# Where the router products stand in query group 0, where weight sums 0 and 1 and the rows are built, and which queue stores the value sums

## The chip, the core and the metric

The kernel runs on one core of one Trainium2 chip. The metric is device time in microseconds of one execution, the median of several. Everything is fp32. A core has a matrix engine (TensorE, PE in the profile), VectorE (DVE), ScalarE (ACT), GpSimd (POOL) and a queue engine (SyncE, SP). Each engine works through its own list of instructions in order; SP, ACT and POOL can also issue DMA transfers, and a transfer that has to wait for its data holds up what stands behind it in that engine's list.

## The reference, cut to what matters

x has 4096 rows of 512, the context 3202 rows of 512. The first part is an attention of the normed rows over the context, whose result, with its products with the rows, is mixed by W_qv; the second is a mixture of experts.

```python
Sim = (hc @ w1)[:, :, None] + (ctx @ w2)[:, None, :] + einsum('bid,bjd->bij', hc * w3, ctx) + b_sim
A = softmax(Sim, axis=2)
hq_hat = einsum('bij,bjd->bid', A, ctx)
Batt = softmax(max(Sim, axis=2), axis=1)
hc_bar = einsum('bi,bid->bd', Batt, hc)
feats = concatenate([hc, hq_hat, hc * hq_hat, hc * hc_bar])
x = x + tanh(g_xattn) * (feats @ W_qv + b_qv)
...
logits = layernorm(x) @ w_router + b_router        # top 2 of 8 experts, capacity 1280
x = x + tanh(g_ffn) * moe(layernorm(x))
```

## The kernel before, in words

Stage 1 does the attention in eight groups of 512 queries (g = 0 to 7). In each group `stage_s` makes the similarities E of all context rows, in six steps jj of two pairs of context tiles each, and keeps a running maximum M on DVE. Products of two by two blocks are done with seven block products instead of eight (`chain`, and `seven` in stage 3), which needs sums of blocks on both sides; DVE builds them. For the keys they are stored to kt_d in group 0 and loaded in later groups; for the values they are stored to vs_d and vd_d (`left_sums`, `build_rest_values`); for the mixing weights W_qv to wt_d (`build_weights(c)`, c = 0 to 3: two loads of wc, the copy of the router columns we into it, a store of wc, four sums wt, a store of wt, both stores on POOL).

At the end of `stage_s` the maximum over all keys is taken: DVE finishes M, PE transposes it in four pieces (mps, L566), DVE reduces it to mt and spreads it on a diagonal (dgm), PE multiplies this with ones (mbps, L159), ACT copies the result to mb, DVE subtracts mb from E (L602), ACT takes the exponent (L603). In groups 1 to 7 the first products of `stage_d(g - 1)`, the mixing of the group before (pad, p6d and so on, with the weights wp loaded from wt_d), stand in this wait on PE.

In group 0 there is no group before. There, 64 router products, W_qv times the centred router weights (we, L289: 128x128 weights, 8 columns), are handed out by the generator `beside`: `behind(mm, beside, n)` issues the next n of them behind the matmul mm. Before the change 12 stand ahead of the transposes, 12 behind them, 24 behind mbps, and the last 16 one by one behind value products. They read W_qv from tiles that borrow the space of others (wq2 lies where xr, the rows of x for the mixing, lies later).

In group 0 the values are not built yet, so `stage_v` multiplies with the plain context tiles: 13 steps j (12 pairs of tiles vc and a rest), each pair with eight products of 512 columns (vv, L677), into four banks. Beside this DVE makes the value sums of step j from vc (vsv), and the store to vs_d goes out from POOL. The tiles vs, wt and vd share a ring of two buffers (tag "vs"), so every third one waits until a store has landed. vc and kt tiles share a ring of five (tag "st"); SP loads them in order. Also in this stage: `stage_n(1)` (statistics of the next queries, after j = 3; POOL stores means to mr_d and loads them back as mrb), `stage_a(1)` (the right side Qp of the next group and its sums), and `stage_z(0)` (ebb and four sums jz). At the end ACT copies the four banks to hqT.

Group 1 then runs `stage_s(1)`, and `rest_rows` (jj = 0), `left_operand` (jj = 1, with the rows xr: four loads, four additions of bqv and a copy of be) and `build_weights(0)` to `(3)` (jj = 1 to 4) are worked in between on DVE. `stage_d(0)`, which needs wt_d, begins at the end of `stage_s(1)`. Before it SP issues 12 zero stores to buf_d.

Stages 2 (routing) and 3 (experts) are not touched.

The order on an engine is mostly set by a planner, which picks by cost and due time; `tc.issue_after(...)` ties an instruction behind another one. The calls around the change are these:

Of the kernel before, what the change touches and what calls it, by code (L numbers as in the profile page):

```python
# [6 lines left out]
F32 = mybir.dt.float32  # L7
I32 = mybir.dt.int32
AF = mybir.ActivationFunctionType
ALU = mybir.AluOpType  # L10
# [4 lines left out]
P = 128  # L15
# [5 lines left out]
def gated_layer(ctx, tc, x, x_t, ctxt, ctxt_t, ctxt_c, ctxt_r, g_xattn, g_ffn, w_sim, w_sim_r, b_sim, W_qv, W_qv_t, b_qv, b_qv_c, w_router, b_router, w1, b1, w2, b2, out):  # L21
# [6 lines left out]
    nc = tc.nc  # L28
# [4 lines left out]
    DC = D // P  # L33
# [90 lines left out]
    with ExitStack() as s1:  # L124
# [218 lines left out]
        def stage_a(g, qT, mrb, last, exp):  # L343

            with tc.issue_after(last.ins):
                tt(qT, qT, mrb[:, 0, :].unsqueeze(1).to_broadcast([P, DC, TG]), ALU.subtract)
            tt(qT, qT, mrb[:, 1, :].unsqueeze(1).to_broadcast([P, DC, TG]), ALU.mult)
            Qp = sb.tile([P, DC, TG], F32, name=f"Qp{g}", tag="Qp")
            with tc.issue_after(exp.ins):
                for c in range(DC):  # L350
                    nc.scalar.activation(
                        Qp[:, c, :], qT[:, c, :], AF.Identity,
                        scale=ws[:, 2 * DC + c : 2 * DC + c + 1], bias=ws[:, DC + c : DC + c + 1],
                    )
                nc.scalar.dma_start(qT_d[g], qT)
            right_sums(g, qT, Qp)
# [33 lines left out]
        def left_sums(name, vc, dst):  # L390

            vs = sb.tile([P, 4, 256], F32, name=f"vs{name}", tag="vs", bufs=2)
            A11, A21, A12, A22 = (vc[:, h, c : c + 256] for h in range(2) for c in (0, 256))
            tt(vs[:, 0, :], A21, A22, ALU.add)
            tt(vs[:, 1, :], vs[:, 0, :], A11, ALU.subtract)
            tt(vs[:, 2, :], A11, A21, ALU.subtract)
            total = tt(vs[:, 3, :], A12, vs[:, 1, :], ALU.subtract)
            nc.gpsimd.dma_start(dst, vs)
            return total
# [5 lines left out]
        def build_rest_values(vc):  # L405
            vd = sb.tile([P, 256], F32, name="vd", tag="vs", bufs=2)
            tt(vd, vc[:, :256], vc[:, 256:], ALU.subtract)
            nc.gpsimd.dma_start(vd_d, vd)

# [78 lines left out]
        def stage_s(g):  # L488
# [8 lines left out]
            for jj, js in enumerate(PAIRS):  # L497
# [28 lines left out]
                if g == 1:  # L526
                    with tc.issue_after(e_add.ins):
                        if live["then"]:
                            live["then"].pop(0)()
                        if 0 < jj <= DC:  # L530
                            build_weights(jj - 1)
                if jj == 4 and 0 < g < NG - 1:
# [23 lines left out]
            if g == 0:  # L556
# [4 lines left out]
                live[g]["pw"] = pw  # L561
            mm = behind(mm, beside, 12)
            ps = ps_tr.tile([P, 4, P], F32, name=f"mps{g}", tag="tr")
            for i in range(4):
                with tc.issue_after(mm.ins):
                    mm = nc.tensor.transpose(ps[:, i, :], M[:, i // 2, 0, (i % 2) * P : (i % 2 + 1) * P], ident)  # L566
            mm = behind(mm, beside, 12)
            mt = sm.tile([P, 4], F32, name=f"mt{g}", tag="mt")
# [3 lines left out]
            with tc.issue_after(mm.ins):  # L572
                mm = diag_rows(ps, f"m{g}", mt)
            live[g]["beside"], live[g]["mm"] = beside, behind(mm, beside, 24)

# [71 lines left out]
        def stage_v(g, early, between):  # L647
# [8 lines left out]
            def product(ps, what, right, start=True, stop=True, rest=None, right_c=None):  # L656
                for i in range(2):
                    vt = load_values(g, what, i, rest)
                    js = list(range(i * JH, (i + 1) * JH)) + ([NJ] if i and rest is not None else [])
                    for j in js:  # L660
                        for b in range(2):
# [4 lines left out]
                            )  # L666

            if g == 0:

                beside, mm = v["beside"], v["mm"]  # L670
                ps = [bank(f"vv{b}") for b in range(DC)]
                for j in range(NJ + 1):
# [9 lines left out]
                    with tc.issue_after(v["last"].ins):  # L682
                        if j < NJ:
                            total = build_values(j, vc)
                        else:
                            build_rest_values(vc[:, 0, :])
                    if j == 2:
                        with tc.issue_after(v["last"].ins):
                            nc.vector.tensor_copy(we, v["pw"])
# [3 lines left out]
                    if j == 5:  # L693
                        early()
                    if j == 8:
                        v["sums"] = total
                assert next(beside, 0) == 0
                for b in range(DC):
# [74 lines left out]
            def left_operand():  # L773
# [8 lines left out]
                v["A"] = {"1": A11, "6": S2, "7": A21, "5": S1, "2": A12, "4": A22, "3": S4}  # L782
                xr = sb.tile([P, 4, 2, BW], F32, name=f"xr{g}", tag="xr")
                for i in range(4):
                    t = 4 * g + i
                    with tc.issue_after(queue[-1].ins):
                        nc.sync.dma_start(xr[:, i, :, :256], x[t * P : (t + 1) * P, :].rearrange("p (j d) -> p j d", j=2))
                    with tc.issue_after(v["last"].ins):
                        tt(xr[:, i, :, :256], xr[:, i, :, :256], bqv.rearrange("p (j d) -> p j d", j=2), ALU.add)
                with tc.issue_after(v["last"].ins):  # L790
                    nc.vector.tensor_copy(
                        xr[:, :, :, 256:],
                        be.rearrange("p (j e) -> p j e", j=2).unsqueeze(1).to_broadcast([P, 4, 2, BW - 256]),
                    )
                v["x"] = xr

            if g:
                rest_rows()
                left_operand()
            else:  # L800

                live["then"] = [rest_rows, left_operand]
# [24 lines left out]
        def stage_z(g):  # L827

            v = live[g]
            ebb = v["ebb"]  # L830
            with tc.issue_after(v["exp"].ins):
                nc.scalar.activation(ebb, ebb, AF.Copy, accum_out=hz[:, g, DC : DC + 1])
# [695 lines left out]
```

## Time and profile before

| | us |
|---|---|
| median of 3 runs | 2652.79 (2651.25 to 2656.39) |
| the profiled execution | 2650.92 |
| its span | 2649.1 |
| PE busy | 2598.4 |
| DVE busy | 1703.0 |
| ACT busy | 458.6 |
| POOL busy | 234.6 |

The span is the time from the first to the last instruction of the profiled execution; the rest of its time lies around it. Busy times of different engines overlap. Times in the timelines are microseconds from the start of the span. In them the wait for maxima of group 0 runs from 94 to 112 us, the value products of group 0 from 112 to 204, the similarities of group 1 from 204 to 282, and the mixing of group 0 begins after that. PE splits each fp32 matmul into two, so 24 router products are 48 lines of the timeline.

### The profile page before, as it was taken

How to read it: one execution, taken by the hardware profiler on the slowest of the kernel's cores; microseconds unless marked ns; L12 is line 12 of the kernel's file. 1: busy time of each engine (PE TensorE's matmuls, PEld its weight loads, DVE VectorE, ACT ScalarE, POOL GpSimd, SP SyncE). 2: the span in 40 equal slices, each digit the busy share in tenths (PEclk: the TensorE clock that was granted, in tenths of full speed). 3: DMA queues.
4: the chain of work that ended last, by engine and by line, in shares of the span. 5: the costliest groups of instructions: out<-in, count | busy, mean ns of one | idle time of the engine just before them, and what ended most of it. 6: DMA issues, size and time to landing. Idle time of an engine off the chain costs nothing. (4 is left out here: it accounts for less than half of the span.)

```text
span 2649.1 us, 29673 instructions
## 1 busy us (share of the span) xinstructions
PE 2598.4 (98%) x11200; PEld 2101.7 (79%) x11200; DVE 1703.0 (64%) x3430; ACT 458.6 (17%) x788; POOL 234.6 (9%) x301
## 2 busy tenths in 40 slices
PE   8999999999999999999999996999999999999998
PEld 7748888888888888888888885777777777777776
DVE  7857856947758578568465566574747565565654
ACT  1201200201102002012020143111111111111111
POOL 0010100000001000000000065010101010101010
PEclk9899999999999999999999997999999999999999
DMA  8576765746746657467446794232314232223210
GB/s 317 175 207 236 217 216 168 242 158 184 251 153 178 242 162 241 169 175 249 149 136 215 271 357 173 74 115 72 128 64 138 95 117 88 104 88 104 76 60 20
DMA packets 178255, 436.06 MB, mean 165 GB/s; under 512 B 17454, under 2 KB 77998, under 8 KB 176064
## 3 DMA queue, kind: packets, MB, share of 16 engines
q1 hardware_dynamic: 150208, 352.25, 40.2%
q0 software_dynamic: 17872, 51.46, 6.1%
q10 hardware_dynamic: 10032, 30.46, 2.9%
q8 instruction: 88, 1.44, 0.2%
q14 instruction: 55, 0.45, 0.1%
HBM read 355.71 MB, written 85.55 MB: 167 GB/s over the span
## 5 line engine op out<-in xcount | busy, mean ns | idle before, releaser
L1276 PE MATMUL pah<-bT,w 128*128 128x320 f32 x512 | 161.1, 437 | 0.5 <-ACT p1h L1283 0.5
L512 PE MATMUL pas<-Qp,kt 128*128 128x256 f32 x672 | 160.3, 380 | 0.0
L662 PE MATMUL pbv<-E,vt 128*128 128x256 f32 x672 | 147.3, 379 | 0.0
L662 PEld LDWEIGHTS pbv<-E,vt 128*128 128x128 f32 x672 | 127.7, 190 | 17.3
L512 PEld LDWEIGHTS pas<-Qp,kt 128*128 128x128 f32 x672 | 127.2, 190 | 17.4 <-issue 0.5
L1276 PEld LDWEIGHTS pah<-bT,w 128*128 128x128 f32 x512 | 98.2, 192 | 40.5 <-ACT p1h L1283 1.4
L602 DVE TENSOR_TENSOR E<-E,mb 128x1024 f32<-128x1024 f32 x96 | 115.2, 1215 | 14.0 <-ACT mb L589 14.0
L603 ACT ACTIVATE E<-E 128x1024 f32<-128x1024 f32 x96 | 101.5, 1058 | 129.3 <-DVE E L602 128.0
L1276 PE MATMUL pao<-w,h 128*128 128x256 f32 x512 | 121.0, 379 | 0.0
L1459 POOL DMA_INDIRECT out<-acc,ti x40 | 40.9, 1022 | 865.1 <-DVE dc L1325 531.2
L1047 PE MATMUL x1p<-W,q2T 128*128 128x264 f32 x512 | 116.1, 387 | 0.0
L1436 PE MATMUL op<-w,h 128*128 128x512 f32 x256 | 114.8, 592 | 0.0
L1276 PEld LDWEIGHTS pao<-w,h 128*128 128x128 f32 x512 | 97.3, 190 | 20.0 <-issue 7.7
L1047 PEld LDWEIGHTS x1p<-W,q2T 128*128 128x128 f32 x512 | 96.7, 190 | 16.1
L468 ACT COPY p1s<-pas 128x512 f32<-128x512 f32 x48 | 28.1, 585 | 437.1 <-issue 257.1
L538 DVE TENSOR_TENSOR M<-M,E 128x1024 f32<-128x1024 f32 x80 | 97.8, 1223 | 4.1
L677 PE MATMUL vv<-E,vc 128*128 128x512 f32 x192 | 88.2, 610 | 0.0
L1436 PEld LDWEIGHTS op<-w,h 128*128 128x128 f32 x256 | 46.6, 190 | 48.7 <-issue 41.4
L1398 DVE TENSOR_TENSOR h<-p4h,u3h 128x320 f32<-128x320 f32 x64 | 31.3, 489 | 78.3 <-PE p4h L1276 78.3
L481 ACT COPY E<-pas 128x512 f32<-128x512 f32 x48 | 28.1, 585 | 306.5 <-PE pas L512 296.7
L1276 PE MATMUL p6h<-x,w1s 128*128 128x320 f32 x256 | 80.2, 436 | 0.0
L512 PE MATMUL pbs<-Qp,kt 128*128 128x256 f32 x336 | 79.7, 380 | 0.3 <-DVE E L479 0.3
(449 smaller groups left out, 5390.3 us busy)
## 6 DMA issues: line engine op xcount, KB each, us to landing
kt<-kt_d SPq DMA_DIRECT2D x84, 896.0 KB, 4.7
w<-in_w SPq DMA_DIRECT2D x32, 2048.0 KB, 9.1
vt<-vs_d SPq DMA_DIRECT2D x56, 768.0 KB, 7.2
wp<-wt_d SPq DMA_DIRECT2D x56, 520.0 KB, 4.6
kt_d<-ktb ACTq DMA_DIRECT2D x12, 896.0 KB, 5.5
buf_d<-zero SPq DMA_DIRECT2D x80, 129.0 KB, 6.0
xb<-buf_d SPq DMA_DIRECT2D x40, 258.0 KB, 6.6
r<-r_d SPq DMA_DIRECT2D x32, 260.0 KB, 6.0
```

The source lines that it names most:

```text
L468: nc.scalar.copy(p1, pa)
L512: nc.tensor.matmul(ps[:, jl, :], kts[j][:, KSLOT[p], k, :], B[p][:, k, :], start=start and jl == 0 and k == 0, stop=stop and k == 1, skip_ ...
L538: tt(M, M, e[:, :, h], ALU.max)
L602: live[g]["last"] = tt(e, e, m, ALU.subtract)
L603: live[g]["exp"] = nc.scalar.activation(e, e, AF.Exp)
L662: nc.tensor.matmul(ps[b], vt[:, j - i * JH, b * P : (b + 1) * P], right(j) if j < NJ else right_c, start=start and j == 0 and b == 0, stop ...
L677: mm = nc.tensor.matmul(ps[b], vc[:, h, b * P : (b + 1) * P], E[j // 2][:, :, h, j % 2, :] if j < NJ else ec, start=j == 0 and h == 0, sto ...
L1047: mm = nc.tensor.matmul(ps[:, j, :B1], qTs[g][:, c, q * P : (q + 1) * P], W1[:, c, j, :], start=(c == 0), stop=(c == DC - 1))
L1276: nc.tensor.matmul(ps, a, b, start=start and i == 0, stop=stop and i == len(A) - 1, skip_group_check=True)
L1398: tt(hi[:, :HC], ps, u, ALU.add)
L1436: nc.tensor.matmul(ps, hT[:, k, 2 * MH :], W2[:, k, :], start=(k == 0), stop=(k == KH - 1))
L1459: sc = nc.gpsimd.indirect_dma_start(out=out[:, :], out_offset=rows_of(ti, s), in_=acc[:, :], in_offset=None, bounds_check=N - 1, oob_is_er ...
```

## The change

Of the 64 router products 6, 7 and 8 stand at the three places of the wait for maxima, and 43 one by one behind the first 43 value products; their result is copied to we after j = 5 instead of j = 2. The rows xr with their bias become a function of their own, which group 0 calls at j = 6 of its value stage (the other groups call it where it stood). `build_weights(0)` and `(1)` are called at j = 7 and 9 of the value stage; `build_weights(2)` and `(3)` at jj = 1 and 2 of group 1. The stores of value sums go out from ACT's queue instead of POOL's. The copy of ebb in group 0 is tied behind the store of qT_d.

```diff
@@ -352,7 +352,7 @@
                         Qp[:, c, :], qT[:, c, :], AF.Identity,
                         scale=ws[:, 2 * DC + c : 2 * DC + c + 1], bias=ws[:, DC + c : DC + c + 1],
                     )
-                nc.scalar.dma_start(qT_d[g], qT)
+                live["sent"] = nc.scalar.dma_start(qT_d[g], qT)
             right_sums(g, qT, Qp)
 
         def build(j):
@@ -395,7 +395,7 @@
             tt(vs[:, 1, :], vs[:, 0, :], A11, ALU.subtract)
             tt(vs[:, 2, :], A11, A21, ALU.subtract)
             total = tt(vs[:, 3, :], A12, vs[:, 1, :], ALU.subtract)
-            nc.gpsimd.dma_start(dst, vs)
+            nc.scalar.dma_start(dst, vs)
             return total
 
         def build_values(j, vc):
@@ -405,7 +405,7 @@
         def build_rest_values(vc):
             vd = sb.tile([P, 256], F32, name="vd", tag="vs", bufs=2)
             tt(vd, vc[:, :256], vc[:, 256:], ALU.subtract)
-            nc.gpsimd.dma_start(vd_d, vd)
+            nc.scalar.dma_start(vd_d, vd)
 
         def build_weights(c):
 
@@ -527,8 +527,8 @@
                     with tc.issue_after(e_add.ins):
                         if live["then"]:
                             live["then"].pop(0)()
-                        if 0 < jj <= DC:
-                            build_weights(jj - 1)
+                        if 0 < jj <= DC - 2:
+                            build_weights(jj + 1)
                 if jj == 4 and 0 < g < NG - 1:
                     ahead[g + 1] = stage_n(g + 1)
                 if jj == 0:
@@ -559,19 +559,19 @@
                 pw = pw.rearrange("p (k c e) -> p k c e", k=4, c=DC)
                 beside = live[g]["we"](pw, [1, 2, 0, 3])
                 live[g]["pw"] = pw
-            mm = behind(mm, beside, 12)
+            mm = behind(mm, beside, 6)
             ps = ps_tr.tile([P, 4, P], F32, name=f"mps{g}", tag="tr")
             for i in range(4):
                 with tc.issue_after(mm.ins):
                     mm = nc.tensor.transpose(ps[:, i, :], M[:, i // 2, 0, (i % 2) * P : (i % 2 + 1) * P], ident)
-            mm = behind(mm, beside, 12)
+            mm = behind(mm, beside, 7)
             mt = sm.tile([P, 4], F32, name=f"mt{g}", tag="mt")
             nc.vector.tensor_reduce(mt, ps, AX.X, ALU.max)
             tt(mt, mt, left[g][1], ALU.max)
             ps = ps_tr.tile([P, 4, P], F32, name=f"mbps{g}", tag="tr").rearrange("p a b -> p (a b)")
             with tc.issue_after(mm.ins):
                 mm = diag_rows(ps, f"m{g}", mt)
-            live[g]["beside"], live[g]["mm"] = beside, behind(mm, beside, 24)
+            live[g]["beside"], live[g]["mm"] = beside, behind(mm, beside, 8)
 
             m = sm.tile([P, 4], F32, name=f"m{g}", tag="mm")
             xw = left.pop(g)[0]
@@ -665,6 +665,22 @@
                                 skip_group_check=True,
                             )
 
+            def rows_and_bias():
+
+                xr = sb.tile([P, 4, 2, BW], F32, name=f"xr{g}", tag="xr")
+                for i in range(4):
+                    t = 4 * g + i
+                    with tc.issue_after(queue[-1].ins):
+                        nc.sync.dma_start(xr[:, i, :, :256], x[t * P : (t + 1) * P, :].rearrange("p (j d) -> p j d", j=2))
+                    with tc.issue_after(v["last"].ins):
+                        tt(xr[:, i, :, :256], xr[:, i, :, :256], bqv.rearrange("p (j d) -> p j d", j=2), ALU.add)
+                with tc.issue_after(v["last"].ins):
+                    nc.vector.tensor_copy(
+                        xr[:, :, :, 256:],
+                        be.rearrange("p (j e) -> p j e", j=2).unsqueeze(1).to_broadcast([P, 4, 2, BW - 256]),
+                    )
+                v["x"] = xr
+
             if g == 0:
 
                 beside, mm = v["beside"], v["mm"]
@@ -684,7 +700,8 @@
                             total = build_values(j, vc)
                         else:
                             build_rest_values(vc[:, 0, :])
-                    if j == 2:
+                    if j == 5:
+                        assert next(beside, 0) == 0
                         with tc.issue_after(v["last"].ins):
                             nc.vector.tensor_copy(we, v["pw"])
                     if j == 3:
@@ -692,9 +709,13 @@
                             ahead[1] = stage_n(1)
                     if j == 5:
                         early()
+                    if j == 6:
+                        rows_and_bias()
+                    if j in (7, 9):
+                        with tc.issue_after(v["last"].ins):
+                            build_weights((j - 7) // 2)
                     if j == 8:
                         v["sums"] = total
-                assert next(beside, 0) == 0
                 for b in range(DC):
                     nc.scalar.copy(hqT[:, b, :], ps[b].rearrange("p a b -> p (a b)"))
                 between()
@@ -780,23 +801,11 @@
                 tt(S4, A12, S2, ALU.subtract)
                 tt(A21, A11, A21, ALU.subtract)
                 v["A"] = {"1": A11, "6": S2, "7": A21, "5": S1, "2": A12, "4": A22, "3": S4}
-                xr = sb.tile([P, 4, 2, BW], F32, name=f"xr{g}", tag="xr")
-                for i in range(4):
-                    t = 4 * g + i
-                    with tc.issue_after(queue[-1].ins):
-                        nc.sync.dma_start(xr[:, i, :, :256], x[t * P : (t + 1) * P, :].rearrange("p (j d) -> p j d", j=2))
-                    with tc.issue_after(v["last"].ins):
-                        tt(xr[:, i, :, :256], xr[:, i, :, :256], bqv.rearrange("p (j d) -> p j d", j=2), ALU.add)
-                with tc.issue_after(v["last"].ins):
-                    nc.vector.tensor_copy(
-                        xr[:, :, :, 256:],
-                        be.rearrange("p (j e) -> p j e", j=2).unsqueeze(1).to_broadcast([P, 4, 2, BW - 256]),
-                    )
-                v["x"] = xr
 
             if g:
                 rest_rows()
                 left_operand()
+                rows_and_bias()
             else:
 
                 live["then"] = [rest_rows, left_operand]
@@ -828,7 +837,7 @@
 
             v = live[g]
             ebb = v["ebb"]
-            with tc.issue_after(v["exp"].ins):
+            with tc.issue_after(v["exp"].ins if g else live["sent"].ins):
                 nc.scalar.activation(ebb, ebb, AF.Copy, accum_out=hz[:, g, DC : DC + 1])
             for c in range(DC):
                 junk = sb.tile([P, 4, P], F32, name=f"jz{g}_{c}", tag="dg").rearrange("p a b -> p (a b)")
```

## The prediction

> **What bounds the kernel now.** I read section 1 of the page first, then the waits of PE, then the timelines of PE, DVE and ACT around the two places that the change touches.
>
> ```profile
> PE 2598.4 (98%) x11200; PEld 2101.7 (79%) x11200; DVE 1703.0 (64%) x3430; ACT 458.6 (17%) x788; POOL 234.6 (9%) x301
> ...
> PE pad L850 <- DMA wp<-wt_d: 4.1, 1, 4.1
> PE pbs L512 <- DVE E L479: 2.7, 3, 2.1
> ```
>
> PE is busy for 98% of the span, so time is won only where PE waits, or where it is busy without getting on. The waits name one stall of each sort here: 4.1 us for the first mixing weights, and 0.3 of the 2.7 us (at 252 us) for E. The other kind hides in the wait for maxima of query group 0. In the timeline of PE (start, length, engine, line, operation; each fp32 matmul counts as two) stands:
>
> ```profile
> 94.39 2.74 PE L289 MATMUL we<-wrc,wq 128*128 128x8 f32 x24
> 96.98 0.64 PE L566 MATMUL mps<-ident,M 128*128 128x128 f32 x4
> 97.46 3.18 PE L289 MATMUL we<-wrc,wq 128*128 128x8 f32 x24
> 100.49 2.05 PE L159 MATMUL mbps<-dgm,ones 128*128 128x512 f32 x2
> 102.34 10.25 PE L289 MATMUL we<-wrc,wq 128*128 128x8 f32 x48
> 112.44 2.06 PE L677 MATMUL vv<-E,vc 128*128 128x512 f32 x2
> ...
> 117.76 1.10 PE L677 MATMUL vv<-E,vc 128*128 128x512 f32 x2
> 118.70 0.28 PE L289 MATMUL we<-wrc,wq 128*128 128x8 f32 x2
> ...
> 131.82 68.91 PE L677 MATMUL vv<-E,vc 128*128 128x512 f32 x160
> ```
>
> The chain that these products stand beside, in the timelines of DVE and ACT (the bracket is the idle time before and its releaser):
>
> ```profile
> 95.21 0.69 DVE L554 TENSOR_TENSOR M<-M,Ec 128x512 f32<-128x512 f32 x1 [1.19 <-ACT Ec L552]
> 97.66 0.69 DVE L569 TENSOR_REDUCE mt<-mps 128x4 f32<-128x512 f32 x1 [1.76 <-PE mps L566]
> ...
> 103.20 13.72 DVE L602 TENSOR_TENSOR E<-E,mb 128x1024 f32<-128x1024 f32 x12 [3.60 <-ACT mb L589]
> 104.46 5.60 ACT L603 ACTIVATE E<-E 128x1024 f32<-128x1024 f32 x5 [1.29 <-DVE E L602]
> ```
>
> M is ready at 95.90 but its transposes start at 96.98, and the diagonal is ready at 99.27 but its product starts at 100.49: PE is in products, in order. The first exponent ends near 105.6, yet the first value product starts at 112.44. The table by stretches (clock and DMA share are the columns before the last) shows why the products take so long:
>
> ```profile
> 97.00:100.50 3.50, 3.50 (x31) 3.50 (x30) 1.87 (x6) 0.00 (x0) 0.38 (x1) 0.87 0.62 235
> 102.50:106.00 3.50, 3.50 (x19) 3.50 (x18) 2.80 (x3) 2.05 (x3) 0.00 (x0) 0.50 0.02 5
> 112.40:116.60 4.20, 4.20 (x9) 2.13 (x9) 4.20 (x4) 3.90 (x4) 0.00 (x0) 0.50 0.16 1
> 116.60:131.80 15.20, 15.20 (x59) 8.51 (x58) 13.67 (x22) 2.63 (x5) 3.08 (x5) 1.00 0.59 185
> ```
>
> From 99.6 to 116.6 the clock is 0.50: 24 products after the diagonal cost 0.42 us each instead of 0.214. The second place:
>
> ```profile
> 286.05 2.56 PE L850 MATMUL pad<-wp,hqT 128*128 128x260 f32 x8 [4.14 <-DMA wp<-wt_d]
> 269.18 0.75 POOL L421 DMA_DIRECT2D wt_d<-wc x1 [8.65 <-DMA buf_d<-zero]
> 273.56 0.78 POOL L428 DMA_DIRECT2D wt_d<-wt x1
> wp<-wt_d SPq DMA_DIRECT2D x1, 520.0 KB, 12.1
> ```
>
> The fourth weight store leaves POOL only at 269 and 273.6. SP's first load of wp goes at 273.8, and needs 12.1 us[...] (mr_d, issued 272.4, landed after 9.8 us).
>
> [...] The trace agrees: half clock for 17.0 us[...], back 4.2 us after the first value product. It also shows that back-to-back 8-column products did not hold the clock. [...] The trace has no vs_d store from ACT; kt_d stores from ACT (896 KB) land in 5.5 us, vs_d from POOL (512 KB) in 5.6.
>
> **Part 1, router products.** 12, 12 and 24 become 6, 7 and 8; 43 instead of 16 follow value products one by one. On the new path:
> - Six products take 12 x 0.107 = 1.28 us, to 95.7; M is there at 95.90, so transposes start at 95.95, 1.03 earlier. DVE's 1.61 us from mt to diagonal gives 98.25.
> - Seven products end at 97.95. The 512-column product starts at 98.3 and, before the clock falls, takes 1.03 (half of the 2.05 shown): done at 99.33, against 102.54.
> - The 3.04 us from there to the end of the first exponent stay: 102.4. Eight products end near 102.2, partly at half clock. Value products start at 102.4, 10.0 us earlier.
> - A pair (value product and router product) costs 1.081 us, from 117.76 to 118.84 and onwards, a value product alone 68.75/80 = 0.859. So a router product is not hidden there: 0.222 us each.
> - If the window edges stay where they were, the clock is back at 106.4: 4.0 us hold 1.9 pairs, then 41.1 x 1.081 = 44.5 and 57 x 0.859 = 49.0. The last value product ends at 199.9 instead of 204.0: **4.1 us gained** (10.0 less 27 x 0.22 = 5.9). [...] the 512-column product can be cold (1 us): 1.9 to 5.3.
>
> **Part 2, weights and rows.** Weight sums 0 and 1, the four xr loads, four additions (0.68 us each) and the small copy leave group 1's products for group 0's value stage. There DVE is busy 38.2 of the 68.2 us from 131.8 on; what comes is 2 x (0.16 + 4 x 0.34) + 2.7 = 6 us. On SP's queue the xr loads stand ahead of vc 7 and the wc loads ahead of vc 8 and 10 (0.6 us each, eight of them), but PE needs a vc tile some 27 us after its slot came free, and a load lands in 4.4. On POOL the four stores stand behind mrb's wait for mr_d; only the ring of two slots (below) waits for them. On PE's path all this costs nothing as long as DVE is done with the right sums and the value sums before PE reaches 199.9. In group 1 only weights 2 and 3 are left, at pairs 1 and 2. Their stores then leave POOL near 235 to 246 instead of 269 to 274, and land (13.9 us at the worst) by 260. The load of wp is then set as in group 2, by the slot of the kt that pair 4 uses: there it was issued at 450.28, 16.2 us ahead of its use at 466.49, and needed 14.0 us, again beside mr_d, so it arrives 2 us early. So the 4.14 us go. The clock also dropped to 0.50 for 3.4 us after this stall: from the first pad to pbd group 1 takes 13.57 us, group 2 12.03, so 1.54 more. With the 0.34 of DVE's lateness: **6.0 us** (bounds: 2.5, if wp is still 2 us late and the clock falls; 6.5).
>
> **Part 3, value stores on ACT.** 13 stores at about 0.33 us of issue each (that of kt_d) go to ACT, which is busy 2.9 of these 68.2 us: nothing. They wait there in order for DVE, behind them Qp, the ebb copy (now behind the qT_d store; only the jz sums need it) and, last, the four hqT copies. POOL loses 13 x 0.71 us and the stores no longer wait behind its wait for mr_d (155.65 to 166.16 before). Against this, DVE now waits for product 43 at about 150.9 (the copy of we) before sums 6. Sums and weights share a ring of two slots: v6, wt0, v9, v10 and vd follow each other in one slot. With 6.5 us per landing and some 8 us of DVE's work I get 152.5 + 4 x 6.5 + 8 = 186.5, 13 us ahead of PE. Price taken: 0; bounds 0 and +16.
>
> **Sum.** 4.1 + 6.0 = 10.1 us. The profiled execution took 2650.92 us (span 2649.1 and 1.8 around it) and would take 2640.8. It stands 1.9 us below the median of 2652.79, which becomes 2642.7; I say **2642.5**. Everything after 300 us should shift unchanged, since PE is the bound there.
>
> **Rivals.**
> - Only the stall goes: the clock returns one or two windows later, or the value products start later than 102.4, and part 1 gives 0 to 2. For it: the window's phase differs from run to run. Against it: the exponents at 1.1 us each keep far ahead of 3.4 us per four value products. 2645 to 2647.
> - Only part 1 is won: wp still meets mr_d, and 2 to 4 us of stall with a fall of the clock remain. For it: the margin in group 2 is only 2 us. 2646 to 2648.5.
> - **Slower**: the two-slot ring. If the four landings were 10 us each, the value sums would end with PE; the hqT copies stand on ACT behind the last store, so each us more holds up group 1. Break-even is at 12.5 us, 0.2% slower at 13.8. At 14, vd comes at 216 and 16 us are lost: 2659. Speaking for it: DVE waited 17.6 us for vs_d landings before, and 4 MB more move in this stage (DMA share 0.70). Against it: the median landing is 5.6, the longest 11.1.
> - The change doesn't do what it says: the order of the built instructions shows 6, 7 and 8 products and then strict alternation, so I give this nothing.
>
> **Chances.** Full sum 0.70, first rival 0.13, second 0.09, a mixture near nothing 0.03, slower 0.05. 0.2% (5.3 us, about what a measurement of this kernel can tell from no change) is 2647.5: faster 0.86, within 0.09, slower 0.05. The range 2638 to 2648.5 takes the full sum's bounds (gain of 5 to 12), the rivals' times, and 2 us of spread between executions.
>
> **What would show it.** Right: transposes near 96.0, value products from 102 to 103, 43 pairs at 1.08 us, the last value product near 200; no wait of PE on wp, no 0.50 clock near 288; DVE's last right sum and vd before 195. Wrong: PE idle before the hqT copies are done, or a first pad that waits; or a start of the value products past 105.

## The result, and the profile after

The changed kernel takes 2643.33 us (median of 7 runs, 2640.88 to 2647.7) against 2652.52 for the kernel before in the same measurement: ratio 0.9966, 95% interval 0.9957 to 0.9975, so 9.2 us faster. The profiled execution took 2643.9, its span 2642.1. One execution of clock_kept (below) was in a slow state, at a granted clock of 0.849 and with 3035.86 us, and is left out.

First the busy times on the page, then the waits of PE (us in total, times, longest):

```profile
PE 2592.5 (98%) x11200; PEld 2096.9 (79%) x11200; DVE 1705.3 (65%) x3430; ACT 458.8 (17%) x788; POOL 228.9 (9%) x288
```

```profile
PE pad L859 <- issue: 2.3, 1, 2.3
PE pbs L512 <- DVE E L479: 1.9, 2, 1.6
...
PE vv L693 <- ACT E L603: 0.5, 1, 0.5
```

The wait of 4.1 us on wp is gone. Three short ones are new: PE now waits for the chain of maxima (0.17 and 0.24 us at the first two places) and for the first exponent. So the products no longer hold the chain up. The timeline of PE:

```profile
93.67 1.40 PE L289 MATMUL we<-wrc,wq 128*128 128x8 f32 x12
95.24 0.66 PE L566 MATMUL mps<-ident,M 128*128 128x128 f32 x4 [0.17 <-DVE M L554]
95.74 1.63 PE L289 MATMUL we<-wrc,wq 128*128 128x8 f32 x14
97.60 1.12 PE L159 MATMUL mbps<-dgm,ones 128*128 128x512 f32 x2 [0.24 <-DVE dgm L158]
98.56 2.71 PE L289 MATMUL we<-wrc,wq 128*128 128x8 f32 x16
101.75 2.07 PE L693 MATMUL vv<-E,vc 128*128 128x512 f32 x2 [0.48 <-ACT E L603]
...
107.18 1.10 PE L693 MATMUL vv<-E,vc 128*128 128x512 f32 x2
108.12 0.28 PE L289 MATMUL we<-wrc,wq 128*128 128x8 f32 x2
...
276.55 1.92 PE L859 MATMUL pad<-wp,hqT 128*128 128x260 f32 x8
```

The first value product starts 8.08 us after the first router product, where it started 18.05 after it before. A pair of value product and router product takes 1.08 us. At 276.55 the first mixing product starts without a wait. In the table by stretches (clock, DMA share and GB/s are the last columns) the half clock ends near 106 instead of 116.6:

```profile
97.00:100.50 3.50, 3.26 (x20) 2.69 (x19) 1.99 (x5) 0.59 (x1) 0.38 (x1) 0.83 0.20 72
102.50:106.00 3.50, 3.50 (x8) 1.68 (x7) 3.50 (x4) 3.26 (x4) 0.49 (x1) 0.50 0.00 0
106.00:109.00 3.00, 3.00 (x11) 1.77 (x12) 3.00 (x4) 2.82 (x6) 1.73 (x2) 0.97 0.00 0
```

DVE and POOL, from their timelines: the value sums of j = 7 waited for a store, the rest's sum vd ended 8 us ahead of PE's end of the stage (199.45), and the last two weight stores left POOL at 239 and 243 instead of 269 and 274.

```profile
163.34 0.43 DVE L394 TENSOR_TENSOR vsv<-vc 128x256 f32<-128x256 f32 x1 [8.59 <-DMA vs_d<-vsv]
...
191.27 0.42 DVE L407 TENSOR_TENSOR vd<-vc 128x256 f32<-128x256 f32 x1
239.40 0.75 POOL L421 DMA_DIRECT2D wt_d<-wc x1 [3.50 <-DVE wc L420]
242.60 0.75 POOL L428 DMA_DIRECT2D wt_d<-wt x1 [2.45 <-DVE wt L427]
```

Two distances on PE serve below as rulers, since only what lies between their ends enters. **A** runs from the first router product to the first product of group 1 (pas): 109.62 before, 105.78 after. **B** runs from that pas to the first pbd of the mixing: 95.61 before, 89.14 after. A gives 3.84 us, B 6.47.

### The profile page after: what moved, and what is told of

It is laid out like the page before. It is cut to its first block, busy times and chain, and to the rows that moved or that the text cites. A ratio compares the mean times of both kernels' runs of the same rounds, so it can differ in the third digit from the quotient of the medians.

```text
span 2642.1 us, 29671 instructions
## 1 busy us (share of the span) xinstructions
PE 2592.5 (98%) x11200; PEld 2096.9 (79%) x11200; DVE 1705.3 (65%) x3430; ACT 458.8 (17%) x788; POOL 228.9 (9%) x288
## 5 line engine op out<-in xcount | busy, mean ns | idle before, releaser
L693 PE MATMUL vv<-E,vc 128*128 128x512 f32 x192 | 94.3, 622 | 0.5 <-ACT E L603 0.5
L512 PE MATMUL p6s<-q,kt 128*128 128x256 f32 x336 | 79.4, 379 | 0.0
```

Of the source, the lines that this page charges most:

```text
L512: nc.tensor.matmul(ps[:, jl, :], kts[j][:, KSLOT[p], k, :], B[p][:, k, :], start=start and jl == 0 and k == 0, stop=stop and k == 1, skip_ ...
L693: mm = nc.tensor.matmul(ps[b], vc[:, h, b * P : (b + 1) * P], E[j // 2][:, :, h, j % 2, :] if j < NJ else ec, start=j == 0 and h == 0, sto ...
```

## The experiments

Times are medians, each with the ratio to the kernel before on the same chip.

| kernel | us | ratio (95%) | half clock in A | A | B |
|---|---|---|---|---|---|
| before | 2652.52 | 1 | 17.1 | 109.62 | 95.61 |
| the changed kernel | 2643.33 | 0.9966 (0.9957 to 0.9975) | 6.8 | 105.78 | 89.14 |
| router_alone | 2649.97 | 0.9985 (0.9978 to 0.9993) | 10.2 | 106.98 | 96.95 |
| router_undone | 2646.45 | 0.9975 (0.9967 to 0.9984) | 17.1 | 109.61 | 89.13 |
| weights_alone | 2647.25 | 0.9976 (0.9967 to 0.9986) | 20.5 | 111.25 | 89.75 |
| pool_stores | 2644.10 | 0.9963 (0.9950 to 0.9976) | 10.2 | 106.84 | 89.13 |
| act_stores_alone | 2651.60 | 0.9992 (0.9984 to 1.0000) | 17.1 | 109.61 | 95.61 |
| means_wide | 2645.65 | 0.9968 (0.9956 to 0.9979) | 23.9 | 112.91 | 90.12 |
| router_all_beside | 2652.69 | 0.9997 (0.9991 to 1.0004) | 10.2 | - | 96.25 |
| after_again | 2645.09 | 0.9968 (0.9957 to 0.9980) | 6.8 | 105.70 | 89.13 |
| clock_kept | 2640.47 | 0.9949 (0.9936 to 0.9961) | 3.4 | 106.19 | 89.13 |
| clock_kept_again | 2641.05 | 0.9952 (0.9938 to 0.9966) | 3.4 | 106.20 | 89.13 |
| clock_kept_more | 2642.48 | 0.9960 (0.9946 to 0.9973) | 0 | 105.40 | 89.13 |
| ring_of_one | 2679.12 | 1.0099 (1.0080 to 1.0117) | - | 112.31 | 119.52 |

Where the table gives the half clock in A, it is a whole number of windows of 3.41 us, from none to seven. Its length differs between executions with the same products there: 17.1 us before, 20.5 in weights_alone. The times are medians over executions, A, B and the half clock those of one. after_again is the changed kernel once more. router_all_beside has no router product ahead of the value products, so it has no A; in ring_of_one the clock also halves at the end of A and inside B (four matmuls of pas take 2.05 us at 205.91, where eight of pbs take 1.89 at 222.13).

### The parts by themselves

router_alone, on the kernel before (the places are ahead of the transposes, behind them, and behind mbps):

```diff
-            mm = behind(mm, beside, 12)
+            mm = behind(mm, beside, 6)
...
-            mm = behind(mm, beside, 12)
+            mm = behind(mm, beside, 7)
...
-            live[g]["beside"], live[g]["mm"] = beside, behind(mm, beside, 24)
+            live[g]["beside"], live[g]["mm"] = beside, behind(mm, beside, 8)
...
-                    if j == 2:
+                    if j == 5:
```

> The kernel before with the router products at 6, 7 and 8 (43 beside value products, we copied after j = 5) and nothing else. Two distances are read from the timeline of PE: A from the first router product to the first product of group 1 (pas), 109.6 us before and 105.8 after the change; B from that pas to the first pbd of the mixing, 95.6 before and 89.1 after. Theory (the parts are separate, each worth what its own place shows): A 105.8 (value products start some 10 us earlier, less 27 x 0.22), B 95.6 with the wait of 4.1 us on wp and a fall of the clock after it; 3.8 us faster than before. Rival (the gain of A needs the stores on ACT, since otherwise the value sums are late for the earlier PE): A 107 or more with PE waiting at the end of the value stage. Rival (the start of the value products is set by the clock or the exponents, not by the products): A 108 to 111.

router_undone, on the changed kernel:

```diff
-            mm = behind(mm, beside, 6)
+            mm = behind(mm, beside, 12)
...
-            mm = behind(mm, beside, 7)
+            mm = behind(mm, beside, 12)
...
-            live[g]["beside"], live[g]["mm"] = beside, behind(mm, beside, 8)
+            live[g]["beside"], live[g]["mm"] = beside, behind(mm, beside, 24)
```

> The changed kernel with the router products back at 12, 12, 24 and 16 (the rest of the change kept). Theory: A 109.6, B 89.1; 6.5 us faster than before, no wait of PE on wp. Rival (the weights are early only because the value stage is early): B 92 to 95, a wait on wp of 1 to 4 us.

weights_alone, on the kernel before:

```diff
-                        if 0 < jj <= DC:
-                            build_weights(jj - 1)
+                        if 0 < jj <= DC - 2:
+                            build_weights(jj + 1)
...
+                    if j in (7, 9):
+                        with tc.issue_after(v["last"].ins):
+                            build_weights((j - 7) // 2)
```

> The kernel before with only weight sums 0 and 1 moved into the value stage of group 0 (and 2 and 3 to pairs 1 and 2 of group 1); value sums still stored by POOL, the rows still in group 1. Theory (wp is late because the fourth weight store leaves POOL at 269): A 109.6, B 89.1 to 89.6; 6 us faster. Rival (the rows' 2.7 us on DVE or the store queue are needed as well): B 91 or more, or A above 110 because the value sums end late behind POOL's wait for mr_d.

By the medians the counts alone give 4.1 us (2654.08 less 2649.97), everything without the counts 7.6 (2654.08 less 2646.45; by the ratio 6.6), the weights alone 6.8. The counts and the weights alone add up to 10.9, against 9.2 for the whole change; the intervals do not tell these apart. Both halves show where the theory put them. The timeline of PE in router_alone and then in weights_alone:

```profile
284.79 3.80 PE L850 MATMUL pad<-wp,hqT 128*128 128x260 f32 x8 [4.49 <-DMA wp<-wt_d]
```

```profile
283.23 1.92 PE L853 MATMUL pad<-wp,hqT 128*128 128x260 f32 x8
```

With the counts alone the stall on wp stays; with the weights alone it is gone, while rows and stores are where they were. So the rows' move and ACT's queue are not needed to remove the stall. Four numbers missed. A of router_alone was 1.2 above the expected value and A of weights_alone 1.6, with 10.2 and 20.5 us of half clock where I had reckoned with 6.8 and 17.1. That A of weights_alone lies above its rival's 110 does not speak for the rival: the rest's sum did end late, at 211.2, but PE waited for nothing in A. B of router_alone was 1.3 longer, since the stall on wp cost two windows of half clock (6.8 us) instead of one (3.4): eight matmuls of pad took 3.80 us behind it, where they took 2.56 before. B of weights_alone was 0.15 above its range and 0.62 above that of the changed kernel: from pas to sc it takes 74.26 us, as before (74.28), and 73.64 with the rows moved too, whether the sums are stored by ACT (router_undone) or by POOL (pool_stores). So these 0.6 us of B are the rows'.

### The queue of the value stores

```diff
-            nc.scalar.dma_start(dst, vs)
+            nc.gpsimd.dma_start(dst, vs)
...
-            nc.scalar.dma_start(vd_d, vd)
+            nc.gpsimd.dma_start(vd_d, vd)
```

> The changed kernel with the value sums stored by POOL again. Theory (the queue is worth nothing as long as DVE ends before PE): value sums 5 wait on POOL behind mrb until about 161 us, the rest sums vd end near 197 instead of 191.7, still ahead of u2s at 203: A 105.8 to 106.5, B 89.1; as fast as the changed kernel within 1 us. Rival (the stores on ACT are what lets the weights into this stage): the chain through the ring of two ends after 203 and PE waits for DVE at the start of group 1: A or B 3 us or more longer than in the changed kernel.

act_stores_alone is the reverse of this edit on the kernel before, with the tie of ebb:

```diff
-            nc.gpsimd.dma_start(dst, vs)
+            nc.scalar.dma_start(dst, vs)
...
-            nc.gpsimd.dma_start(vd_d, vd)
+            nc.scalar.dma_start(vd_d, vd)
```

> The kernel before with only the value stores on ACT (and the ebb copy behind the store of qT_d). Theory (worth nothing, PE is never waiting for them): A 109.6 with 1.5 us to either side for the window of the clock, B 95.6; within 1.5 us of before. The last value sum ends some us earlier than at 192. Rival (freeing POOL lets the weight stores of group 1 go earlier): B 94 or less. Rival (ACT held up by a store that waits delays Qp or the hqT copies): A 112 or more.

pool_stores is as fast as the changed kernel (0.9963 against 0.9966 and 0.9968), and act_stores_alone has the A and B of the kernel before to within 0.01 us, its time 0.08% lower with an interval that ends at 1. The queue is worth nothing on PE's path here. What it buys is margin. In the timeline of DVE, pool_stores:

```profile
202.03 0.42 DVE L407 TENSOR_TENSOR vd<-vc 128x256 f32<-128x256 f32 x1 [2.92 <-DMA vs_d<-vsv]
```

The rest's sum comes at 202 (expected: 197) instead of 191, just after PE's end of the stage at 201.4 (A is 0.3 above its range, with one window of half clock more than in the changed kernel, 10.2 us against 6.8). On POOL the value store that stands behind mrb left at 161.87 (expected: about 161), since POOL had waited 10.05 us for the store of means to land. No one waited for it, because on POOL nothing that PE needs stands behind its store; the hqT copies are on ACT.

### The late ring, forced

```diff
-            vs = sb.tile([P, 4, 256], F32, name=f"vs{name}", tag="vs", bufs=2)
+            vs = sb.tile([P, 4, 256], F32, name=f"vs{name}", tag="vs", bufs=1)
...
-            wt = sb.tile([P, 4, BW], F32, name=f"wt{c}", tag="vs", bufs=2)
+            wt = sb.tile([P, 4, BW], F32, name=f"wt{c}", tag="vs", bufs=1)
```

(vd, w23 and prb, which share the tag, likewise.)

> The changed kernel with one buffer instead of two in the ring that value sums, weight sums and the rest share. This forces the case of the slower rival: twelve value sums, two weight sums and the rest each wait for the landing of the one before, some 6.5 + 1.6 us, from about 119 on. Theory (PE waits once this chain is late: for context tiles that the sums still hold, for the right sums of group 1, and for the hqT copies behind the last store on ACT): the rest's sum ends near 235 to 245 instead of 191.7, A 135 to 150, the kernel 25 to 45 us slower than the changed one. Rival (nothing on PE hangs on the chain): A 106 to 108, less than 2 us slower.

34.0 us slower than the changed kernel in the same measurement, vd at 240.9: both as expected. The place was not: A grew by 6.5 only, not to 135 or more, and B by 30. The waits of PE:

```profile
PE pas L512 <- DMA kt<-kt_d: 12.0, 2, 7.0
PE pbs L512 <- DVE E L479: 10.8, 3, 9.7
```

The value products themselves never starved; of the 6.5 us, 5.0 are the first wait for kt, between the last of them and pas. The late sums hold the vc tiles, so the key tiles kt, which take over their slots, are loaded late; and ACT's copies for group 1 stand behind the stores that wait for DVE (ACT waited 15.0 us for vd). That is the slower rival of the prediction, with the kt loads as a second road to PE that I had not named.

### Why wp was late

means_wide writes the means untransposed, so the means loaded back are not the right ones; on the kernel before:

```diff
-            nc.gpsimd.dma_start(mr_d[g].rearrange("k i p -> p k i"), mr)
+            nc.gpsimd.dma_start(mr_d[g].rearrange("k i p -> (k i p)").rearrange("(p a) -> p a", a=8), mr.rearrange("p k i -> p (k i)"))
```

> The kernel before, but the store of means writes eight neighbouring words per partition (128 runs of 32 bytes) instead of transposing into 1024 single words; so the means that are loaded back stand in the wrong places, and what is computed from them differs. Theory (wp is late for two reasons, its issue at 273.8 and the 12.1 us of its landing, and the second is the crawl of the single-word store beside it): mr_d lands in 3 to 5 us instead of 10, wp in 5 to 6, near 279, ahead of its use at 281.9: no wait on wp, B (pas of group 1 to the first pbd) 89.5 to 90 instead of 95.6, without any move of the weights; about 6 us faster. A (first router product to pas) 109.6 as before. Rival (the landing is long because of the zero stores and the weight stores queued ahead): wp still lands after 284, B 93 or more.

The store of means in the kernel before, from the DMA issues from 272 to 287 us (KB each, median us to landing at the end; it was issued at 272.38):

```profile
mr_d<-mr POOLq DMA_DIRECT2D x1, 4.0 KB, 9.8
```

In means_wide, the first load of wp in the timeline of SP, and the DMA issues from 275 to 284 us:

```profile
276.45 0.32 SPq L847 DMA_DIRECT2D wp<-wt_d  x1
```

```profile
wp<-wt_d SPq DMA_DIRECT2D x4, 520.0 KB, 6.0
...
mr_d<-mr POOLq DMA_DIRECT2D x1, 4.0 KB, 2.4
```

The same 4 KB land in 2.4 us instead of 9.8, and the first load of wp, the one that PE had waited for, in 5.3 instead of 12.1. It was issued at 276.45, later than the 273.80 before, with the weights still built in group 1, and the wait on it is gone all the same; B is 90.12. So the stall had two halves, and taking either away is enough: the late issue, which the change took away, and the slow landing. A is 112.91 where 109.6 were expected, with two windows of half clock more (23.9 us against 17.1). That the total gain is 8.2 us, more than B alone, I leave open: means are stored in every group, and wrong means change the routing.

### The price of a router product

router_all_beside has 0, 0 and 0 in the wait for maxima, on the kernel before (the three counts change alike; the first is shown):

```diff
-            mm = behind(mm, beside, 12)
+            mm = behind(mm, beside, 0)
...
-                    if j == 2:
+                    if j == 8:
```

> The kernel before with none of the 64 router products in the wait for maxima, all of them one by one beside value products (we copied after j = 8). Theory (nothing hides a product there): value products start as with 6, 7 and 8, some 8.2 us after the end of the last sc product, but 64 x 0.222 = 14.2 us are added to 86 of value products: the stretch from the start of the value products to pas of group 1 is 100.1 plus 2 to 3.5 for the half clock, 4.7 longer than with 43 beside; in all as long as before within 2 us. Rival (products beside value products are nearly free once the clock is up, their cost being that of the first ones at half clock): the stretch stays near 97.7 and the kernel is 4 us faster than before.

The timeline of PE:

```profile
97.85 2.08 PE L159 MATMUL mbps<-dgm,ones 128*128 128x512 f32 x2 [1.71 <-DVE dgm L158]
102.95 2.07 PE L677 MATMUL vv<-E,vc 128*128 128x512 f32 x2 [3.02 <-ACT E L603]
```

PE is idle for 3.0 us ahead of the value products, and they start 8.9 us after the end of the last sc product (at 94.09), against 7.9 in the changed kernel; the 1.0 us is that of mbps, which took 2.08 us at half clock here and 1.12 there. So taking all products away starts the value products no earlier than 6, 7 and 8 do. From there to pas are 102.74 us (expected 102.1 to 103.6) against 97.70 in the changed kernel, so 21 more products cost 5.0 us, 0.24 each. Of this 0.4 us is half clock behind the start (5.1 us of it against 4.4), which leaves 0.22 each, the price that the prediction had used. The kernel takes as long as the one before (0.9997).

### The clock

clock_kept, on the changed kernel:

```diff
+                def dense(mm):
+
+                    with tc.issue_after(mm.ins):
+                        return nc.tensor.matmul(dm, ident, live[0]["qT"][:, 0, :], start=True, stop=True)
...
-            mm = behind(mm, beside, 7)
+            mm = dense(mm)
+            mm = behind(mm, beside, 3)
...
-            live[g]["beside"], live[g]["mm"] = beside, behind(mm, beside, 8)
+            live[g]["beside"], live[g]["mm"] = beside, behind(dense(mm), beside, 8)
```

> The changed kernel with two extra dense 512-column products in the wait for maxima (identity times normed queries, into a bank that nothing reads; they add to what is computed and change nothing of it), one ahead of 3 instead of 7 router products behind the transposes, one ahead of the 8 behind mbps; so 47 beside value products. Theory (the clock falls because 8-column products don't count as busy, and 6.8 us at half clock cost 3 us of the value stage and the wait): with half of each window dense the clock stays at 1.0, value products start 8.1 us after the first router product as before, at full speed, A 105.8 - 2.1 + 4 x 0.22 = 104.6; about 1 us faster than the changed kernel. Rival (half a window is not enough to hold the clock): the half-clock stretch is there as before, A 106.5 to 108.5.

clock_kept_more changes this to:

```diff
-            live[g]["beside"], live[g]["mm"] = beside, behind(dense(mm), beside, 8)
+            live[g]["beside"], live[g]["mm"] = beside, behind(dense(dense(mm)), beside, 4)
...
-                    if j == 5:
+                    if j == 6:
```

> As the kernel with two dense extra products, but with two of them behind mbps and 4 instead of 8 router products there: 51 beside value products, we copied after j = 6. Theory (the window from mbps to the first value products decides): more than half of it dense, the clock stays at 1.0 throughout, which saves the 1.7 us that were still lost; 4 x 0.22 = 0.9 more beside the value products: A 105.4, about 0.8 us faster than with two. Rival (the 1.7 us were the phase of the window, not its content): A 107, 0.9 us slower than with two.

> The kernel with two dense extra products once more, since its interval and that of the changed kernel overlap. Theory (a shorter half-clock stretch in the value stage, 1 to 3 us): 0.9945 to 0.996 of before, A between 104.6 and 106.2. Rival (its first timing was luck): 0.9965 or more, with A 106 to 107.

> The changed kernel itself once more, beside the next two on one chip. A (first router product to pas of group 1) 105.8 or, with the window of the clock elsewhere, up to 107; B (that pas to the first pbd) 89.1; 9 to 10 us faster than before.

With dense products in the wait there was less half clock: 6.8 us in A without any, 3.4 with two (from 103.1 and 103.8 in the two executions of clock_kept), none with three. A different place of the windows does not explain the first step. The windows lie in a grid of 3.41 us, which each execution's clock record gives. In the two profiled executions of the changed kernel a window ends 5.67 and 5.50 us after the first router product, and the clock falls there; in those of clock_kept one ends at 5.66 and 5.65, the clock holds, and falls one window later. The timelines of PE in clock_kept and then in clock_kept_more:

```profile
98.91 1.02 PE L572 MATMUL dm<-qT,ident 128*128 128x512 f32 x2
99.77 1.85 PE L289 MATMUL we<-wrc,wq 128*128 128x8 f32 x16
102.10 1.12 PE L706 MATMUL vv<-E,vc 128*128 128x512 f32 x2 [0.48 <-ACT E L616]
```

```profile
98.12 1.88 PE L572 MATMUL dm<-qT,ident 128*128 128x512 f32 x4
99.83 0.95 PE L289 MATMUL we<-wrc,wq 128*128 128x8 f32 x8
101.31 1.12 PE L706 MATMUL vv<-E,vc 128*128 128x512 f32 x2 [0.52 <-ACT E L616]
102.27 0.28 PE L289 MATMUL we<-wrc,wq 128*128 128x8 f32 x2
```

What failed in clock_kept is the expectation that half of each window was dense. Its second dense product stands mostly ahead of the window from 99.7 to 103.1, in which products of 128 columns or more fill 1.25 of the 3.41 us; the clock fell at its end. In clock_kept_more they fill 2.10 us of the window from 99.3 to 102.8, and it held. But this window ends 0.45 us later after the first router product, and by an estimate from these figures clock_kept would have had 1.25 + 0.45 = 1.7 us at that place. Windows with 1.67 us (before, from 1461.5) and 1.68 us (the changed kernel, from 2632.0) kept the clock. So one execution does not separate the third product from the place of the window, which was the rival. That 8-column products do not count as busy stays a guess: 3.41 us of mostly such products (before, 96.18 to 99.60) did not hold the clock, and more than that no run shows.

A of clock_kept_more is 105.40, as worked out; but the expected order of the two in time is not shown (0.9960 against 0.9949 and 0.9952, intervals that overlap). A of clock_kept is 106.2, above the 104.6 expected and 0.4 above that of the changed kernel: four more products beside value products cost 0.9 us, and 1.0 us less of half clock among the value products gives back only 0.5. The medians of clock_kept are 2 to 5 us below those of the changed kernel (ratios 0.9949 and 0.9952 against 0.9966 and 0.9968), with intervals that overlap. It is the fastest kernel tried, but its lead does not arise in this wait. At the transposes of the last group its two profiled executions are 0.5 us behind those of the changed kernel (1258.5 us from the first router product against 1258.0). Then the clock stays up at the last mixing, where the changed kernel loses 6.8 us to half clock in both executions, which gives 2.3 us, and stages 2 and 3, which no edit touches, are 1.9 to 2.6 us shorter. Whether the dense products do more there than shift the work against the windows, no run tests.

## Why the prediction was right

- **Part 1.** Worked out 4.1 us, A shows 3.84. Step by step, measured from the first router product: transposes at 1.57 (worked out 1.56), the 512-column product at 3.93 (3.91), the first value product at 8.08 (8.0). The clock came back 4.4 us after that (4.0), and a pair costs 1.08. That it fits so closely is in part luck with the windows: in router_alone and pool_stores, with the same counts and one window of half clock more, A gives 2.6 and 2.8 us, which is within the 1.9 to 5.3 that I had estimated. router_alone and router_undone separate this part, and router_all_beside confirms its price from the other side.
- **Part 2.** Worked out 6.0, B shows 6.47. From the start of sc to the first pad: 7.76 before, 3.46 after, so 4.30 (4.14). From the first pad to pbd: 13.57 against 12.04, so 1.53 (1.54). The rest, from pas to sc, is 0.64, where the term had 0.34. The first load of wp was issued at 260.3, 16.2 us ahead of its use, as forecast. One reading was off: the 14.0 us taken from group 2 are those of the second load, issued at 451.14; the first needed 12.2, so the margin there was 4 us and not 2. The reason given, late issue and the crawl of mr_d together, stood the test of means_wide (12.1 us to land against 5.3); how the one transfer slows the other is not shown.
- **Part 3.** Zero was right. The step under it was mis-sized: I put vd at 186.5, with 6.5 us for each landing; it came at 191.3. The store of sums 5 was issued at 149.3, beside the store of means (issued at 147.6, waited for until 160.6), and sums 7 waited 8.6 us for it. I had seen this crawl for wp, and in the 11.1 us of the one vs_d store that went beside mr_d before, and not carried it to the ring; so the margin was 8 us and not 13. No run separates the means from the other transfers of this stretch. A store on ACT also took 0.52 us to issue, not 0.33, at no cost.
- **Sum.** 10.1 against 9.2 measured. That everything after 300 us shifts unchanged was not quite so. At the first pbd the profiled execution was 11.0 us ahead (0.7 of them won before the router products), and at the last group's transposes still 11.0 (1362.74 against 1351.70). In the span 7.0 are left. Of the 4.0 lost, 3.0 go at the last mixing. PE waits 2.3 us there in both kernels, but in both profiled executions of the changed kernel the windows fell so that the clock halved for 6.8 us; from the first pad to the next stage it took 27.60 instead of 24.62. The timelines of PE before and after:

```profile
1466.25 3.75 PE L850 MATMUL pad<-wp,hqT 128*128 128x260 f32 x16 [2.29 <-issue]
```

```profile
1455.22 6.73 PE L859 MATMUL pad<-wp,hqT 128*128 128x260 f32 x16 [2.29 <-issue]
```

The other 1.0 goes in stages 2 and 3. So one such place moves an execution by more than the 2 us of spread that the range allowed for, and that the sum came so near the measured gain is in part luck: A and B alone show 10.3.

- **The rivals.** The first came in part: in router_alone and pool_stores the clock returned one window later and the value products started 1.0 us later than in the changed kernel, but 2.6 and 2.8 us of part 1 were left, not 0 to 2. The second did not come, wp was there in time. The slower one is real, but needs the ring to be much later than it was.

## What to carry to other kernels

A matmul engine that is busy all the time can still be off its path (here it was busy for 98% of the span, before and after): filler work placed in a wait is free only until the awaited value is there, and its excess delays everything behind it (here by 10 us, the start of the value products at 18.05 against 8.08 us). Count filler to the length of the wait, put the rest where its price is known (here 0.22 us each), and check whether the filler keeps the clock up (here 3.41 us of mostly 8-column products did not). When a load comes late, look both at when it is issued and at what else is moving then (here 12.1 us to land beside the single-word store of means, 5.3 beside the one in runs of 32 bytes).

## What the runs showed of the hardware

- PE's clock, from the clock records and the times of PE's products. In the kernel before and the changed kernel, each stretch at half clock that ends before the program does is a whole number of 3.41 us: 17.07, 3.41 and 30.72 us before, 6.83, 6.83 and 27.31 after. What the windows of 3.41 us at whose end the clock fell, or held, contain:

| kernel | window | PE busy, us | in products of 128 columns or more, us | at its end the clock |
|---|---|---|---|---|
| before | 96.18 to 99.60 | 3.41 | 0.64 | fell to 0.50 |
| before | 280.50 to 283.92 | 1.40 | 1.40 | held |
| before | 283.92 to 287.33 | 1.28 | 1.28 | fell to 0.50 |
| before | 1461.52 to 1464.93 | 2.45 | 1.67 | held |
| the changed kernel | 95.93 to 99.34 | 3.17 | 1.12 | fell to 0.50 |
| the changed kernel | 1451.02 to 1454.43 | 1.91 | 1.13 | fell to 0.50 |
| the changed kernel | 2632.03 to 2635.45 | 1.68 | 1.68 | held |

The first two rows differ most: the clock fell after a window in which PE was busy throughout, mostly with 8-column products, and held after one in which it was busy for 1.40 us, all of it in wide ones. At half clock it came back after windows with 3.30 us (before, from 113.25) and 3.26 us (the changed kernel, from 102.75) of wide products, and did not after one with 2.90 us (before, from 1642.42). These are single windows of two executions; they give no threshold, and why the clock fell or held, no run shows.

- The store of means as 1024 single words took 9.8 us to land in group 1 (9.5 to 12.1 over the seven groups), as 128 runs of 32 bytes 2.4. Over the seven groups POOL waited 65.2 us for it to land before and 10.9 us in means_wide. The 520 KB load of wp issued just after it in group 1 took 12.1 us in the one case and 5.3 in the other.
